# A graph layer on one core: sums stored by SyncE, a fifth of the tables resident, gathers of successive edges with narrow one-hots

## The chip, the cores and the metric

The kernel runs on one core of a Trainium2 chip. Its time is what the device takes for one execution, in microseconds (us). Eight executions of the kernel before took 15392.79 to 15410.78 us, with a median of 15401.63 us. Engines are named as in the profile: PE is TensorE (PEld its weight loads), DVE is VectorE, ACT is ScalarE, POOL is GpSimd, SP is SyncE.

## The reference, cut to what matters

```python
h = jnp.maximum(_layernorm(x, axis=-1), 0.0)           # x is [100000, 64]
local, nbr = h[dst], h[src]                            # 3.3 million edges, sorted by dst
y = concatenate([local, nbr - local]) @ W.T + b
s = segment_sum(y, dst); cnt = segment_sum(ones, dst)
out = x + where(cnt > 0, s / max(cnt, 1), 0)
```

There are 3,300,000 edges (1.6 million both ways and one loop per node), some 33 for each node. Since the layer is linear, what has to be computed per node is the sum of `h[src]` over its edges and their number. The rest is a product with the weights, node by node.

## The kernel before, in words

**First stage (L274 to L310, up to 437 us).** The layer norm is computed for 28 columns of nodes at a time. Each row of h is written as three bf16 parts and ones (194 numbers, 388 bytes) to a table in HBM, `h3` (`h` in the profile). The output's own part goes to `hb`, and zeros go to `acc`, which is to hold the sums (65 numbers a node: 64 sums and the count). `bounds` (L242) finds the smallest destination of every chunk (`base_f`, `base_b`, `base_i`, `base_r`) and flags a chunk whose destinations span 128 or more.

The edges are then summed in two ways, side by side.

**Chunks (`chunks`, L345).** A chunk is 128 x 28 successive edges of the sorted list, 28 on each partition. For each of the 28 columns POOL gathers 128 rows of `h3` by an indirect DMA (L391, `nb<-h,si`). DVE makes one-hots of the edges' destinations, 14 columns at a time and 128 wide (`one_hot`, L340, `hot<-near`), and PE multiplies them (L396, `ps<-nb,hot`), so that the 28 matmuls of a chunk sum its edges by node. DVE takes the sums to SBUF (L407, L409), and POOL adds them to `acc`: by an indirect DMA ahead of the loop (L366), by a direct one at a register's row in the loop (L371). Indices come 16 chunks at a time (`si`, `di`, L352 and L354, by SP), from which DVE makes `rel`, `near` and `to` (L356 to L361).

**Windows (`sort_lane`, `fill_lane`, `quads`).** 256 windows of 7968 edges each, of fewer than 256 nodes, are sorted by source, 128 windows at a time, one on each partition (`sort_lane`, L418: ACT copies, DVE takes minimum and maximum, L455 to L457). `fill_lane` gathers each window's pieces by source block (L636, L721) and writes the positions to HBM (`sr_d`, `dt_d`, `et_d`, `xs_d`). `quads` (L740) takes four windows at once, and 64 quads in all. A quad is 158 steps, one for each of 157 blocks of 640 nodes and one for the end. For each block:

- SP loads the table of `h3`, three blocks in one transfer of 727.5 KB (L761, `tab<-tables`, three buffers), and for each eight blocks the positions (L752 `srs`, L756 `dt`), issued eight steps ahead
- DVE makes the one-hots of two blocks at once: `gh` (L789), which picks rows out of the block, and `dh` (L340), which puts them to their nodes
- PE picks (L811, `gp<-tab,gh`, 6 matmuls a block), ACT casts the rows (L813, `gs`), PE puts them (L819, `total<-gs,dh`, 16 matmuls of 32 rows a block)

At the quad's end ACT copies the totals (L835), DVE adds the windows' own rows (L767 and L839) and reduces (L843, L845), and POOL adds four tiles of 256 nodes to `acc` (L849).

**Order.** Each engine and each queue is served in order. `chunks` is a generator: the code of the sort and of the quads takes one step of it, one gather, as often as a running account says. The account charges `GATHER` = 1250 ns for a gather and credits what the other work is taken to last: in the sort each piece's own estimate, in the four quads ahead of the loop 2 x `STEP` = 2100 ns for two steps. An addition is not issued at once but put into `later`, and issued 56 gathers after its sums are computed (`LAG`), and not sooner than `GAP` = 8 gathers after the one before it. `add_now(True)` issues all that are left.

**Loop (L909).** Four quads (`U0`) run ahead of the loop, beside `fill_lane`. The loop makes three passes of 20 quads (`SB`) and 98 chunks (`KB`). 58 chunks (`PA`) come ahead of it.

**After the loop** the flags decide on a slow path, which is not taken here (L937, L947), and the last stage reads `acc`, divides, multiplies by the weights and writes the output (L990 to L1019).

## Time and profile before, and how to read it

| | |
|---|---|
| median of 8 runs | 15401.63 us |
| profiled execution | 15381.45 us, its span 15379.7 us |
| first gather of a chunk | 437 us |
| sort, up to the first quad | 437 to 2585 us |
| four quads ahead of the loop, and the chunks left over | 2585 to 3686 us |
| the three passes of the loop start at | 3686, 7482 and 11268.5 us |
| end of the last addition in the loop | about 15050 us |
| bytes moved | 4097.9 MB, of which the tables are 3328 x 727.5 KB and 64 x 242.5 KB |

The profile shows one execution. A group is one line's instructions on one engine: their number, the time in which at least one of them ran, the mean of one, and the idle time of the engine ahead of them with what ended it. "issue" is time in which the engine waited for nothing that the profile shows. In the forty slices each digit is a share in tenths, 9 being 90% or more. The ends of matmuls are modelled, and a register load or a DMA issue does not count as busy.

### The profile page before, as it was taken

To read this page: it belongs to the slowest core of one execution; us is meant where nothing else is said; L and a number is where in the kernel's file an instruction comes from. 1 tells how busy PE (TensorE), PEld (TensorE's weight loads), DVE (VectorE), ACT (ScalarE), POOL (GpSimd) and SP (SyncE) were. 2 spreads that over 40 slices of the span, in tenths; PEclk is the share of its full clock that TensorE was granted. 3 is DMA by queue.
4 is the path that set the end of the run, shared out by engine and by line. 5 is a ranking of instruction groups with operands and counts; after the bars stand their busy time and mean duration, and the time that the engine had idled before them with its cause. 6 is when DMAs were issued, how large, how long until landed. Compare 5 with 4: busy or idle time off the path is not lost. (4 is left out here: it accounts for less than half of the span.)

```text
span 15379.7 us, 559362 instructions
## 1 busy us (share of the span) xinstructions
PE 11558.4 (75%) x238778; PEld 9478.5 (62%) x238778; DVE 11312.0 (74%) x15452; ACT 6112.6 (40%) x11710; POOL 11130.6 (72%) x11210
## 2 busy tenths in 40 slices
PE   6101001596999989998799998989979999998885
PEld 5100001475777777777677777777767777777775
DVE  6889797675777777777677777777767777777774
ACT  5335344242444444444344444444434444444441
POOL 4776766546777777777777777777777777777776
PEclk7555555798999999999899999999989999999997
DMA  7683233796999999999899999999989999999997
GB/s 295 123 104 55 48 51 76 183 311 214 319 315 308 309 304 311 309 311 305 265 310 321 314 317 304 311 307 310 308 262 310 319 313 313 313 309 308 307 306 280
DMA packets 1746424, 4097.89 MB, mean 266 GB/s; under 512 B 943899, under 2 KB 952230, under 8 KB 1738950
## 3 DMA queue, kind: packets, MB, share of 16 engines
q1 hardware_dynamic: 1182534, 3461.26, 64.7%
q0 software_dynamic: 454208, 535.92, 17.1%
q10 hardware_dynamic: 107168, 64.74, 2.4%
q8 instruction: 1877, 30.75, 0.8%
q14 instruction: 637, 5.22, 0.1%
HBM read 3880.72 MB, written 219.04 MB: 267 GB/s over the span
## 5 line engine op out<-in xcount | busy, mean ns | idle before, releaser
L391 POOL DMA_INDIRECT nb<-h,si x9856 | 9425.9, 956 | 3298.2 <-issue 2812.3
L813 ACT CAST gs<-gp 128x386 bf16<-128x386 f32 x10048 | 4837.6, 482 | 7092.0 <-PE gp L811 6867.8
L811 PE MATMUL gp<-tab,gh 128*128 128x193 bf16 x60288 | 6236.8, 251 | 989.2 <-DMA tab<-tables 614.8
L811 PEld LDWEIGHTS <-gh 128*128 128x128 bf16 x60288 | 4893.7, 99 | 2012.0 <-issue 942.4
L340 DVE TENSOR_TENSOR dh<-dt,c 128x1024 bf16<-128x1024 int16 x5056 | 3450.9, 683 | 2857.0 <-PE total L819 2726.5
L789 DVE TENSOR_TENSOR gh<-srs,c 128x1536 bf16<-128x1536 int16 x5056 | 4762.1, 942 | 19.5 <-PE gp L811 17.2
L819 PE MATMUL total<-gs,dh 32*128 32x193 bf16 x160768 | 4417.6, 247 | 36.5 <-issue 34.1
L819 PEld LDWEIGHTS <-dh 32*128 32x128 bf16 x160768 | 3196.9, 94 | 1049.3 <-issue 1029.2
L396 PE MATMUL ps<-nb,hot 128*128 128x193 bf16 x9856 | 1802.2, 263 | 2456.7 <-DVE sums L409 1876.2
L396 PEld LDWEIGHTS <-hot 128*128 128x128 bf16 x9856 | 973.7, 104 | 2433.6 <-DVE sums L409 1925.7
L455 ACT COPY tmp<-keys 128x1536 f32<-128x1536 f32 (+14 forms) x540 | 650.1, 1214 | 1239.8 <-DVE keys L457 1014.5
L456 DVE TENSOR_TENSOR keys<-tmp,keys 128x1536 f32<-128x1536 f32 (+14 forms) x540 | 756.9, 1422 | 90.6 <-ACT tmp L455 89.2
L340 DVE TENSOR_TENSOR hot<-near,c 128x1792 bf16<-128x1792 int16 x704 | 759.9, 1080 | 9.6 <-PE ps L396 9.5
L457 DVE TENSOR_TENSOR keys<-tmp,keys 128x1536 f32<-128x1536 f32 (+14 forms) x540 | 756.6, 1421 | 2.3
L849 POOL DMA_DIRECT2D acc<-wsums x256 | 348.0, 1359 | 185.1 <-DVE gh L789 62.7
L636 POOL DMA_INDIRECT kf<-ksort,at_i x322 | 310.1, 963 | 98.8 <-issue 88.9
L371 POOL DMA_DIRECT2D acc<-sums x294 | 301.8, 1027 | 15.1 <-DMA acc<-wsums 7.5
L407 DVE TENSOR_REDUCE sums<-ps 128x64 f32<-128x192 f32 x352 | 123.5, 351 | 149.1 <-PE ps L396 148.3
L839 DVE SCALAR_TENSOR_TENSOR whole<-own,whole 128x193 f32<-128x193 bf16 x512 | 191.3, 415 | 40.3 <-ACT whole L835 39.3
L303 PEld LDWEIGHTS o_ps<-w_own,hT 128*128 128x128 f32 x784 | 156.3, 254 | 79.7 <-ACT hT L298 69.8
L366 POOL DMA_INDIRECT acc<-sums,to x58 | 94.7, 1632 | 148.4 <-DVE sums L409 128.0
L721 POOL DMA_INDIRECT kx<-ksort,xat x128 | 120.8, 943 | 110.5 <-DVE xat L718 56.9
(174 smaller groups left out, 3577.7 us busy)
## 6 DMA issues: line engine op xcount, KB each, us to landing
tab<-tables SPq DMA_DIRECT2D x3328, 727.5 KB
srs<-sr_d SPq DMA_DIRECT2D x1216, 512.0 KB
nb<-h,si POOLq DMA_INDIRECT x9856
tables<-h ACTq DMA_DIRECT2D x157, 242.5 KB
h<-parts SPq DMA_DIRECT2D x28, 1358.0 KB
acc<-zeros SPq DMA_DIRECT2D x28, 910.0 KB
at<-acc SPq DMA_DIRECT2D x28, 910.0 KB
xt<-in_x SPq DMA_DIRECT2D x28, 896.0 KB
```

The lines of the kernel that those rows point to most:

```text
L340: nc.vector.tensor_tensor(out.rearrange("p k (a d) -> p k a d", d=D), numbers[:, :, None].to_broadcast(shape), upto[:shape[0], :n].rearran ...
L391: last[POOL] = nc.gpsimd.indirect_dma_start(out=nb[:, j], out_offset=None, in_=h3, in_offset=bass.IndirectOffsetOnAxis(ap=si[:, u, at:at + ...
L396: nc.tensor.matmul(ps, lhsT=before[0][:, j], rhs=before[1][:, j, :CE], start=before[2] == 0 and j == 0, stop=before[2] == parts - 1 and j ...
L455: last[ACT] = nc.scalar.copy(tmp, lo)
L456: nc.vector.tensor_tensor(lo, tmp, hi, ALU.min)
L457: last[DVE] = nc.vector.tensor_tensor(hi, tmp, hi, ALU.max)
L636: last[POOL] = nc.gpsimd.indirect_dma_start(out=kf[:, c], out_offset=None, in_=ksort, in_offset=bass.IndirectOffsetOnAxis(ap=at_i[:, c0 + ...
L789: nc.vector.tensor_tensor(gh[:, :m].rearrange("p c i b s -> p (c i) b s"), srs[u, s // SL][:, c:c + m].rearrange("p c i s -> p (c i) s")[: ...
L811: nc.tensor.matmul(gp[:, i], lhsT=ghots[t][:, i, b], rhs=row[:, b + i * (NB - NR), :CE], start=b == 0, stop=b == NR - 1)
L813: nc.scalar.copy(gs[t], gp)
L819: nc.tensor.matmul(total[:, i, to(b)], lhsT=hot[at, b * P:b * P + P], rhs=of[at], start=flags.get("start", False) and b == 0, stop=flags.g ...
L849: nc.gpsimd.dma_start(acc[ds(at, CH)].rearrange("(b p) c -> p b c", p=P), sums, accum_op=ALU.add)
```

## The change

- **Sums.** The sums of a tile of nodes are no longer added to `acc` but stored there, by SP. Two neighbouring tiles can share one node, the first of the later tile; so, ahead of the store of the next tile, SP copies that row from `acc` to a side table (`side_c`, `side_w`). After the loop the 5 tiles of side rows are added by indirect DMAs. The sums of the first three chunks (`EARLY`) stay in SBUF, and are added after the loop. `GAP` is 4.
- **Resident tables.** Every fifth table transfer (`KEEP`), 11 of 53, is made once ahead of the loop into SBUF, and the quads of the loop take these from there.
- **Gathers and one-hots.** A gather takes 128 successive edges of the sorted list (`by_gather`, on the host, which only lays out the inputs), not every 28th. Their destinations lie close together and move on by about 4 nodes a gather, so the one-hot is 32 columns wide (`BAND`), compared after the drift of 4 nodes a column is taken off, and it stands in a wider tile of zeros. PE's matmul reads 128 columns of that tile, as before. `bounds` flags a chunk whose destinations leave the band.
- **Numbers.** `KB` is 94 in place of 98, so 70 chunks come ahead of the loop in place of 58; `STEP` 1300 in place of 1050, and 350 ns more credit for each piece of the second sort (`EXTRA`); indices come 8 chunks at a time (`KG`).

The diff, cut to its core:

```diff
-KB = 98
+KB = 94
-KG = 16
+KG = 8
-STEP = 1050
-GAP = 8
+STEP = 1300
+GAP = 4
+BAND = 32
+EARLY = 3
+EXTRA = 350
+KEEP = 5
...
         def bounds(m):
             nc.vector.tensor_reduce(least[:n, m:m + 1], d[:n], axis=AX.X, op=ALU.min)
+            nc.vector.tensor_tensor(e[:n].rearrange("c (p j) -> c p j", j=J), d[:n].rearrange("c (p j) -> c p j", j=J),
+                                    drift_i[:n, None, :].to_broadcast([n, P, J]), ALU.subtract)
...
-            nc.vector.tensor_reduce(most[:n, m:m + 1], d[:n], axis=AX.X, op=ALU.max)
+            nc.vector.tensor_reduce(off[:n, 0, m:m + 1], e[:n], axis=AX.X, op=ALU.max)
...
+            nc.vector.tensor_reduce(off[:n, 1, m:m + 1], e[:n], axis=AX.X, op=ALU.min)
...
                 nc.vector.tensor_sub(rel[:, :k], di[:, :k], base_b[:, at][:, :, None].to_broadcast([P, k, J]))
+                nc.vector.tensor_sub(rel[:, :k], rel[:, :k], drift[:, None, :].to_broadcast([P, k, J]))
...
-            def addition(q, rows_to, sums):
-                if dynamic is None:
-                    nc.gpsimd.indirect_dma_start(
-                        out=acc, out_offset=bass.IndirectOffsetOnAxis(ap=rows_to, axis=0),
-                        in_=sums, in_offset=None, compute_op=ALU.add)
-                else:
-                    at = number(base_r[0:1, ds(dynamic + q, 1)], POOL, V)
-                    nc.gpsimd.dma_start(acc[ds(at, P)], sums, accum_op=ALU.add)
+            def keep(q, sums):
+                c = ds(first + q if dynamic is None else dynamic + q, 1)
+                after = ds(first + q + 1 if dynamic is None else dynamic + q + 1, 1)
+                def put():
+                    at = number(base_r[0:1, c], SP, V)
+                    last[SP] = nc.sync.dma_start(acc[ds(at, P)], sums)
+                def shared():
+                    at = number(base_r[0:1, after], SP, V)
+                    last[SP] = nc.sync.dma_start(side_c[c], acc[ds(at, 1)])
+                add_later((LAG - 1) * J, put)
+                add_later((LAG - 1) * J + GAP, shared)
+            narrow = [[few.tile([P, JH * (P + D) + JH * D], BF16, name=f"hot{part}{i}") for i in range(2)]
+                      for part in range(J // JH)]
+            for hot in narrow[0] + narrow[1]:
+                nc.vector.memset(hot, 0.0)
...
-                    hot = rows.tile([P, JH, P], BF16, name="hot", bufs=4)
+                    hot = narrow[part][q % 2]
...
-                        one_hot(hot, near[:, u, part * JH:part * JH + JH], P)
+                        one_hot(hot[:, part * JH * D:][:, :JH * (P + D)].rearrange("p (k x) -> p k x", x=P + D)[:, :, :BAND],
+                                near[:, u, part * JH:part * JH + JH], BAND)
...
-                        nc.tensor.matmul(ps, lhsT=before[0][:, j], rhs=before[1][:, j, :CE],
+                        nc.tensor.matmul(ps, lhsT=before[0][:, BAND // 2 + j * P:BAND // 2 + j * P + P], rhs=before[1][:, j, :CE],
...
-                if s < NCB and s % TG == 0:
+                if s < NCB and s % TG == 0 and kept is not None and s // TG % KEEP == 0:
+                    tabs[u, s // TG] = kept[:, s // TG // KEEP]
+                elif s < NCB and s % TG == 0:
...
-                    def addition(w=(base + u) * W + i, sums=sums):
-                        at = number(wb_r[0:1, ds(w, 1)], POOL, V - CH)
-                        nc.gpsimd.dma_start(acc[ds(at, CH)].rearrange("(b p) c -> p b c", p=P), sums, accum_op=ALU.add)
-                    add_later((LAG - 1) * J, addition)
+                    keep(u, i, sums)
+            def keep(u, i, sums):
...
+                def put():
+                    at = number(wb_r[0:1, w], SP, V)
+                    last[SP] = nc.sync.dma_start(acc[ds(at, CH)].rearrange("(b p) c -> p b c", p=P), sums)
+                def shared():
+                    at = number(wb_r[0:1, after], SP, V + P)
+                    last[SP] = nc.sync.dma_start(side_w[w], acc[ds(at, 1)])
+                add_later((LAG - 1) * J, put)
+                add_later((LAG - 1) * J + GAP, shared)
...
-                        gathers(ns)
+                        gathers(ns + (EXTRA if l else 0))
...
+                kept = stay.tile([P, -(-NTB // KEEP), TG, NB, CT], BF16, name="kept")
+                for k in range(0, NTB, KEEP):
+                    m = min(TG, NCB - k * TG)
+                    nc.sync.dma_start(kept[:, k // KEEP, :m].rearrange("p c b f -> p (c b f)"),
+                                      tables[k][:, :m].rearrange("p c x -> p (c x)"))
...
-                    for _ in quads(U0 + g * SB, SB):
+                    for _ in quads(U0 + g * SB, SB, kept):
...
+                for q, sums in enumerate(early):
+                    at = number(base_r[0:1, q:q + 1], POOL, V)
+                    nc.gpsimd.dma_start(acc[ds(at, P)], sums, accum_op=ALU.add)
...
+        for k in range(SETS * W // P):
+            add_side(k, side_w, wb_d, 0, P)
+        for k in range(NMT):
+            add_side(k, side_c, base_i.rearrange("m p -> (m p)")[:, None], 0 if k else EARLY, min(P, NCH - 1 - k * P))
```

`add_side` loads 128 side rows and their nodes, and adds them to `acc` by one indirect DMA of POOL. Small checks of the tiles' order go into the flags (a handful of DVE instructions on one partition).

## The prediction

> **What bounds the kernel now.** I read the page first, then one pass of the loop by groups and by waits, then a few microseconds of it in order of time.
>
> The page: the share of each engine, then forty slices of the span.
>
> ```profile
> span 15379.7 us, 559362 instructions
> PE 11558.4 (75%) x238778; PEld 9478.5 (62%) x238778; DVE 11312.0 (74%) x15452; ACT 6112.6 (40%) x11710; POOL 11130.6 (72%) x11210
> ...
> DMA  7683233796999999999899999999989999999997
> ```
>
> No engine is above 75%, and yet the DMA row stands at 9 from the eleventh slice on: that is the loop (L909), three passes over 20 quads each, from 3686 us to about 15050 us, 11364 us of 15380. A pass is bounded by what never stops in it, so I took the middle one, from its first gather at 7482 us to the first gather of the next at 11268.5 us, and its groups on POOL (count, then busy us, mean ns, then idle us ahead of them):
>
> ```profile
> L391 POOL DMA_INDIRECT nb<-h,si x2744 | 2617.4, 954 | 847.6 <-issue 780.7 <-DMA nb<-h,si 21.3 <-PE gp L811 18.3
> L849 POOL DMA_DIRECT2D acc<-wsums x80 | 108.6, 1357 | 56.7 <-DMA acc<-wsums 20.2 <-DVE dh L340 17.7 <-DVE gh L789 16.2
> L371 POOL DMA_DIRECT2D acc<-sums x98 | 100.7, 1028 | 4.9 <-DMA acc<-wsums 2.4 <-DVE sums L409 2.3
> L778 POOL DMA_INDIRECT rows_x<-h,xs x40 | 38.6, 965 | 12.2 <-issue 11.9 <-DMA nb<-h,si 0.3
> ```
>
> Busy and idle of these four groups add to 3786.7 us, the whole pass: POOL never waits for anybody (the idle before a gather is 0.3 us of its own issue), so 72% busy is POOL at its limit. One gather costs (2617.4 + 847.6 - 12.0 for the one wait on its indices) / 2744 = 1.258 us.
>
> PE is the neighbour. The waits of the same pass (us in total, times, longest):
>
> ```profile
> PE gp L811 <- DMA tab<-tables: 175.2, 198, 3.6
> PE ps L396 <- DMA nb<-h,si: 113.1, 68, 40.7
> ...
> DVE rel L356 <- DMA di<-in_dst_p: 42.4, 7, 8.2
> ...
> PE ps L396 <- DVE sums L409: 34.7, 43, 3.0
> ...
> PE gp L811 <- DVE gh L789: 27.0, 12, 6.1
> ```
>
> PE is busy 3388.9 of the 3786.5 us. It waits for POOL's gathers only 113 us, 41 of them once, at the top of the pass. So if POOL were free, PE would gain some 72 us inside the pass and no more: the two are nearly tied, and what the change gives PE counts as much as what it takes from POOL. PE's rows in order of time (start, length):
>
> ```profile
> 6009.81 1.15 PE L811 MATMUL gp<-tab,gh 128*128 128x193 bf16 x6 [3.06 <-DMA tab<-tables]
> ...
> 6012.47 2.12 PE L811 MATMUL gp<-tab,gh 128*128 128x193 bf16 x12
> ...
> 6015.89 1.19 PE L811 MATMUL gp<-tab,gh 128*128 128x193 bf16 x12
> ...
> 6017.96 1.19 PE L811 MATMUL gp<-tab,gh 128*128 128x193 bf16 x12
> ...
> 6020.03 1.19 PE L811 MATMUL gp<-tab,gh 128*128 128x193 bf16 x12
> ...
> 6022.02 1.19 PE L811 MATMUL gp<-tab,gh 128*128 128x193 bf16 x12
> ```
>
> Undisturbed, two steps take 2.07 us (1.99 with one chunk matmul among them instead of two): 1580 pairs at about 2.05 are 3239 us, PE's floor in a pass. The row at 6012.47 is stretched from 1.19 to 2.12 us because DVE put a chunk's one-hot between the two it makes for PE; DVE's own row, with its 1.08 us:
>
> ```profile
> 6013.19 1.08 DVE L340 TENSOR_TENSOR hot<-near,c 128x1792 bf16<-128x1792 int16 x1
> ```
>
> **The change, part by part, for one pass.**
>
> Sums. The 80 + 98 additions leave POOL: 108.6 + 56.7 + 100.7 + 4.9 = 271 us. Four chunks fewer are 112 gathers, 141 us. POOL is left with 2632 x 1.258 = 3311, rows_x 51, the 12 us on the indices, together 3374 us, and what follows the last gather. There the seven last additions now run one after the other, each waiting for the one before, from 11234.3 to 11256.4 us: 22 us, 3.2 each. In their place stand two transfers for each sum, a store and a copy of the next tile's first row out of the same tensor, on SP, each behind the other: 14 x 3.2 = 44 us. POOL's sum is 3418 us.
>
> On SP a sum costs two register loads and two issues. The own-row loads (L767) have the same form and follow each other every 1.28 us, so 348 items are 445 us of SP, which is busy with its instructions about a quarter of the loop and otherwise waits for PE to free a table buffer. Queued behind a waiting store or copy are the table, srs, dt and index loads, and PE waits for the tables. A copy must wait until its store has landed, the next store until the copy has. Bounds: nothing, if each wait falls into SP's idle time (items are at least 4 gathers, 5.0 us, apart, and an addition lands in about 3.2 us); 3.2 + 1.28 us for every item, 1559 us, if none does. I take 25 us, because the spacing is longer than the landing.
>
> The Trainium skill, "DMA: Bandwidth & Descriptors", section Queues, rings and completion order, says that a queue's descriptors are taken in ring order on each engine. It speaks against this part: POOL's additions had a queue of their own, and the stores line up behind the tables. A table of 727.5 KB at the 307 GB/s of this pass takes 2.4 us, so by that rule an item lands after some 5.6 us, not 3.2, and the 5.0 us of spacing leaves 0.6 us x 348 = 209 us of SP waiting in a pass. The trace of before has no such store, so it cannot decide.
>
> Tables. 33 of 157 blocks stay (11 of 53 loads of a quad): 20 x 33 x 242.5 KB = 164 MB of the pass's 1161, 14%. Three buffers of three steps each mean that a load may take two tables' time, 6 steps or 6.2 us; a resident table among them makes it 9.3 us, and that holds for three loads of four. Of the 42 loads left in a quad about 10.5 keep the short cover, against 53 now: 175.2 x 10.5 / 53 = 35 us. Bounds 0 and 175; I take 45.
>
> The Trainium skill, "TensorE: Matmul & The Clock Gate", section Part 1: The HAM clock gate, has an idle array run at half rate until about 3.4 us of work have passed. The row at 6009.81 fits: after 3.06 us of idle six matmuls take 1.15 us, which take 0.68 elsewhere. By that rule each long table wait that goes would give back up to 1.7 us more; I add nothing for it.
>
> One-hots. The rows of the same helper are 683 ns for 1024 columns, 1080 for 1792 and 1480 for 2560, so about 0.52 ns a column and 150 ns fixed; 14 x 32 = 448 columns are 0.38 us. DVE then makes dh, gh and hot in 0.68 + 0.94 + 0.38 = 2.0 us, inside PE's 2.05. The stretch of 2.12 - 1.19 = 0.93 us goes, 196 times: at most 182 us, at least nothing, since DVE catches up in the next pair; half, 91. The sums that stand behind a hot come sooner: of 34.7 us 20 go, of the 27 on gh 17.
>
> Chunks. 112 matmuls fewer at 0.08 us are 9. Index loads double in number, 7 to 12, at 6 us of wait each (42.4 / 7), half the bytes: +25 us. The order of edges inside a gather changes neither its count nor its bytes.
>
> PE's sum: busy 3388.9 - 9 - 91 = 3289. Idle is 398 now; tables -130, gathers -72, sums -20, gh -17, index +25 leave 184. With 22 us more at the pass's end: 3495. POOL has 3418, so **PE is late next**. I add the 25 us for SP: **3520 us a pass**, against 3788 on the mean now: 3 x 268 = -804 us.
>
> Before the loop. 336 gathers more, 423 us of POOL. The 58 indirect additions go (95 us busy, 148 idle ahead of them on the page): -243. In the first four quads POOL waits 224 us for PE's buffers, and the larger STEP puts gathers there. That leaves -44. DVE, which is 89% busy in the sort, saves 85 x 0.70 us less 13 new at 0.38, 54 us, and spends some 25 us more on the bounds at the start. I take -30; from -110 to +120, if the gathers left over at the end of the quads (195 us by their number, 156) don't overlap.
>
> After the loop: three additions kept back and five indirect ones for the first rows, each behind the other at 3.2 us, with their loads: 8 x 3.2, and some 20 us for loads and small DVE work: +45 us. The resident tables are loaded in the first quads, 8 MB, where DMA has room: 0.
>
> Sum: 15381.45 us of the profiled execution (its span 15379.7) - 30 - 804 + 45 = 14592. The median of the eight runs is 20 above that execution: **14610 us**.
>
> **The rivals.**
>
> POOL stays the bound (chance 0.17). For it: its row has no idle at all, and PE's waits may shrink more than I take. Then a pass is 3418 us, 102 less than mine: 14300 us.
>
> The cover doesn't pay (0.15). SP's new work in front of the tables eats the longer cover, and the one-hots' stretch was caught up anyway. PE keeps 175 us on tables and the 91: 3520 + 130 + 91 = 3741 less what POOL's tie no longer adds, about 3700: 15150 us. Against it: the DMA row loses 14% of its bytes.
>
> SP becomes the chain (0.15), the way to a slower kernel. Store and copy alternate on one in-order queue with the tables behind them. If an item delays a table by more than 268 / 348 = 0.77 us on the mean, and PE feels it, the gain of a pass is gone. At 1.5 us it is 522 a pass instead of 25: 3520 + 497 = 4017, 16100 us. Against it: SP idles three quarters of the loop.
>
> No difference (0.03): the gains and SP's delay cancel. That the change isn't in force is excluded: the program of the changed kernel has no addition of POOL in the loop and 14 x 32 columns in its one-hots.
>
> **The numbers.** My forecast has 0.50, by itself 14400 to 14900. A difference of 0.2% (31 us) is about what a measurement of this kernel can tell. Faster: 0.50 + 0.17 + 0.15 = 0.82; same 0.03; slower 0.15. The range takes in the first three: 14250 to 15300.
>
> **What would show it.** Right: no POOL addition in the loop, POOL with waits on PE's buffers (nb <- PE ps) of some 100 us a pass, hot at 0.38 us, table waits under 60 us a pass, pairs still at 2.07 us. Wrong: SP rows that wait long on acc; table waits as before or larger; POOL still without idle; or a gather that no longer costs 1.258 us, from which half of my sum hangs.

## The result, and the profile after

The changed kernel takes 15436.49 us (median of 12 runs, 15392.53 to 15489.95), the kernel before 15399.64 us (33 runs beside them, 15388.63 to 15410.92): a ratio of **1.0024, 95% interval 1.0017 to 1.0031**. I had said 14610. Where the 0.24% comes from, stage by stage, from the two spans:

| stage | before, us | after, us | difference | forecast |
|---|---|---|---|---|
| up to the first pass of the loop | 3686.5 | 3974.9 | +288 | -30 |
| three passes | 11364 | 11082 (3684.5, 3696.8, 3700) | -282 | -804 |
| after the loop | 330 | 355 | +25 | +45 |
| span | 15379.7 | 15411.7 | +32 | -789 |

So the change does bring something in each pass, 94 us and not 268, and loses all of it ahead of the loop. The page of the changed kernel, engines and slices:

```profile
span 15411.7 us, 562939 instructions
PE 11531.1 (75%) x238778; PEld 9533.2 (62%) x238778; DVE 10917.2 (71%) x15549; ACT 6106.8 (40%) x11710; POOL 10315.1 (67%) x10611
...
DMA  7494223686688888888788888888878888888887
```

POOL went from 72% to 67%, and the DMA row in the loop from 9 to 8: both reliefs came. The middle pass (7659.4 to 11356.2 us), POOL's gathers of the chunks (count, then busy us, mean ns, then idle us ahead of them and what ended it):

```profile
L424 POOL DMA_INDIRECT nb<-h,si x2632 | 2484.5, 944 | 1139.4 <-issue 760.2 <-DMA si<-in_src_p 145.3 <-PE gp L849 134.7
```

Beside these POOL has only the 40 rows_x. The additions are gone, and POOL, which waited for nobody before, now waits for its indices and for PE. It is not the bound any more: its last gather of the pass ends at 11259.0 us, 66 us ahead of PE's last quad (11325.5). Before, it ended 12 us behind it (11234.3 and 11222.0). PE's waits in the same pass (us in total, times, longest):

```profile
PE gp L849 <- DMA tab<-tables: 185.9, 122, 6.5
PE gp L849 <- DVE gh L827: 46.2, 24, 5.7
```

The first line matters most. A fifth of the tables is never loaded, and still PE waits for tables 186 us, against 175. It waits less often (122 times, not 198) and longer at a time (6.5 us, not 3.6). For the gathers it waits 45 us (113 before), for the sums 20 (35). Who holds the loads up stands in the waits of SP's own queue in that pass:

```profile
SPq L799 <- PE gp L849: 859.9, 478, 6.4
SPq L788 <- DVE gh L827: 581.6, 263, 10.3
...
SPq L396 <- DMA acc<-sums: 105.4, 43, 5.4
SPq L893 <- DMA side_w<-acc: 101.6, 35, 5.0
SPq L897 <- DMA acc<-wsums: 48.6, 31, 4.2
```

The first line before:

```profile
SPq L761 <- PE gp L811: 1686.6, 828, 12.6
```

This wait is harmless: a table load (L799) that waits for PE to free the buffer is a load that is early. Spread over 840 loads in place of 1061, SP's lead fell from 1.6 to 1.0 us a load. The second is a load of `srs` that waits for its buffer, 447 us before; rival R-b below is about it. The last three are new: a copy that waits for its store to land, and a store for its copy, 109 waits and 256 us a pass. One of the longest table waits, SP's queue in order of time:

```profile
9031.59 0.92 SPq L897 DMA_DIRECT2D side_w<-acc  x1
9037.82 0.42 SPq L893 DMA_DIRECT2D acc<-wsums  x1
9038.29 1.92 SPq L799 DMA_DIRECT2D tab<-tables  x2
```

and PE beside it:

```profile
9037.58 0.68 PE L849 MATMUL gp<-tab,gh 128*128 128x193 bf16 x6
9044.75 1.15 PE L849 MATMUL gp<-tab,gh 128*128 128x193 bf16 x6 [6.50 <-DMA tab<-tables]
```

A copy is issued until 9032.5 us. The store behind it waits until 9037.8 us for the copy's 260 bytes to land, 5.3 us, one of the longest such waits. Two table loads stand behind that store and go out at 9038.3 us and after, and PE, which reached the table at 9038.3, gets it at 9044.75.

### The profile page after: what moved, and what is told of

Same layout as the page of the kernel before. It is cut to its first block, busy times and chain, and to the rows that moved or that the text cites. A ratio compares the mean times of both kernels' runs of the same rounds, so it can differ in the third digit from the quotient of the medians.

```text
span 15411.7 us, 562939 instructions
## 1 busy us (share of the span) xinstructions
PE 11531.1 (75%) x238778; PEld 9533.2 (62%) x238778; DVE 10917.2 (71%) x15549; ACT 6106.8 (40%) x11710; POOL 10315.1 (67%) x10611
## 5 line engine op out<-in xcount | busy, mean ns | idle before, releaser
L849 PE MATMUL gp<-tab,gh 128*128 128x193 bf16 x48408 | 5055.5, 252 | 1112.5 <-DMA tab<-tables 690.6
L849 PE MATMUL gp<-kept,gh 128*128 128x193 bf16 x11880 | 1241.2, 249 | 6.9 <-DVE gh L827 3.6
L363 DVE TENSOR_TENSOR hot<-near,c 128x448 bf16<-128x448 int16 x704 | 267.7, 381 | 76.5 <-PE ps L429 76.4
L321 PE MATMUL o_ps<-w_own,hT 128*128 128x128 f32 x784 | 196.7, 388 | 16.2 <-ACT hT L316 15.5
L305 POOL TENSOR_TENSOR sq<-xt,parts 128x1792 f32<-128x1792 f32 x28 | 98.6, 3525 | 162.7 <-ACT parts L304 162.7
L1106 DVE TENSOR_TENSOR yt<-y_ps,ht 128x512 f32<-128x512 f32 x112 | 65.5, 620 | 176.5 <-POOL ht L1093 122.7
```

Source lines behind the costliest of these rows:

```text
L321: nc.tensor.matmul(o2[:, i], lhsT=hT[:, i], rhs=w_own.rearrange("p a c -> p (a c)"), start=False, stop=True)
L363: nc.vector.tensor_tensor(out.rearrange("p k (a d) -> p k a d", d=D), numbers[:, :, None].to_broadcast(shape), upto[:shape[0], :n].rearran ...
L849: nc.tensor.matmul(gp[:, i], lhsT=ghots[t][:, i, b], rhs=row[:, b + i * (NB - NR), :CE], start=b == 0, stop=b == NR - 1)
```

## The experiments

Theory T1: in the loop, the stores and copies stand in SP's program ahead of the table loads and delay them, which takes away what the resident tables give. (Comparing in the traces, load by load, when PE's last matmul freed the buffer with when SP issued: in the loop of the kernel before 9% of the loads came more than 0.2 us late, by 0.25 us on the mean over all; in the changed one 40%, and 1.2 us.) The rivals: R-a, the short cover of a load next to a resident table makes the waits; R-b, a load of `srs` or `dt` that waits for its buffer does; R-c, the waits are only where PE shows slack that POOL sets. For the loss ahead of the loop: the order in which gathers are issued, or their number, or the one-hots and checks.

Of 18 runs 13 fell on chips where the kernel before took 24511 to 24857 us in place of 15375 to 15384, and there PE waited on its own issue; the last section tells of them. Their times do not bear on the theories. The readings that follow are from the other five. The rows are from the middle pass of each.

**1. The sums back on POOL, all else as changed.**

```diff
-                    at = number(wb_r[0:1, w], SP, V)
-                    last[SP] = nc.sync.dma_start(acc[ds(at, CH)]..., sums)
+                    at = number(wb_r[0:1, w], POOL, V)
+                    nc.gpsimd.dma_start(acc[ds(at, CH)]..., sums, accum_op=ALU.add)
...
-                add_later((LAG - 1) * J + GAP, shared)
```

(the same for the chunks; `GAP` is 8 again, and no side rows are added after the loop)

> The changed kernel, but the sums are added by GpSimd as before: no stores and no copies on SyncE in the loop, no side rows after it, GAP 8. Resident tables, narrow one-hots and the numbers stay. Theory T1 (the store and copy items stand in SyncE's queue ahead of the table loads, so that 41% of the loads are issued late and the waits on tables stay at 186 us a pass): the waits gp<-tab fall to 60 us a pass or less, and GpSimd, which gets 271 us back, becomes the bound at 3374 + 271 = about 3650 us a pass, 50 less than the 3700 of the changed kernel; total 15436 - 150 - 20 (nothing after the loop) + some 20 for the 70 indirect additions ahead of the loop that GpSimd cannot hide = about 15300. Rival R-a (the waits belong to the shorter cover of the load that stands last before a resident table, and to the landing time itself): the waits stay at 150 to 190 us, as in both kernels. Rival R-b (a load of srs or dt that waits for its buffer at the head of the queue holds the tables): the waits stay at 150 or more.

There it took 24702.85 us, 0.9933 of the kernel before, and nothing follows. Run again:

> The same kernel as in e4_pool_sums (the changed kernel with the sums added by GpSimd as before), because the chip of that run took 24857 us for the kernel before, with TensorE waiting on its own issue, and so could not tell the theories apart. The expectation is unchanged: T1 has the waits gp<-tab at 60 us a pass or less and GpSimd as the bound at about 3650 us a pass, total about 15300; R-a and R-b have the waits on tables at 150 to 190 us. If TensorE waits on its issue again, nothing follows.

15202.27 us, ratio 0.9885 (0.9868 to 0.9901); passes 3622 and 3626 us. PE's wait on tables in the second:

```profile
PE gp L844 <- DMA tab<-tables: 13.9, 21, 2.4
```

and POOL's groups in the same pass:

```profile
L419 POOL DMA_INDIRECT nb<-h,si x2633 | 2511.8, 954 | 818.9 <-issue 748.1 <-DMA nb<-h,si 21.6 <-DMA si<-in_src_p 17.8
L888 POOL DMA_DIRECT2D acc<-wsums x80 | 109.0, 1363 | 43.0 <-DVE gh L822 16.9 <-DMA acc<-wsums 10.6 <-DVE hot L363 4.6
L392 POOL DMA_DIRECT2D acc<-sums x94 | 96.5, 1026 | 4.9 <-DMA acc<-wsums 2.5 <-DVE sums L438 2.2
```

Table waits fall from 186 to 14 us, and 7% of the loop's loads are issued more than 0.2 us late, not 40%: resident tables do pay when no item stands ahead of the loads. R-a and R-b would have kept the waits; both are out as the main cause (the loads of `srs` even wait longer for their buffer, 677 us in the pass). With rows_x (51 us) POOL's rows add up to the pass again, to within 9 us, and its last gather ends 12 us behind PE's last quad: POOL is the bound, as forecast (3650), and PE waits 159 us for gathers. A gather costs (2511.8 + 818.9 - 17.8) / 2633 = 1.258 us, as before. Note what this pass says of the tables: of the 160 us it is shorter than before, 141 are the 112 gathers that were moved out of it. Where POOL is the bound, 160 us less waiting for tables buys next to nothing.

**2. A fourth table buffer, and STEP 1800.** Two edits in one kernel. STEP acts ahead of the loop alone; the fourth buffer serves the loop and the four quads ahead of it.

```diff
-                    tabs[u, s // TG] = tab = load.tile([P, TG, NB, CT], BF16, name="tab")
+                    tabs[u, s // TG] = tab = load.tile([P, TG, NB, CT], BF16, name="tab", bufs=4)
-STEP = 1300
+STEP = 1800
```

> The changed kernel with two edits that act in different stages: four table buffers in place of three (the loop), and STEP 1800 in place of 1300 (the four quads ahead of it). Loop: T1 has a table loaded 3.1 us sooner, so that a delay of 1.0 us on the mean in SyncE's queue no longer reaches TensorE: waits gp<-tab under 60 us a pass in place of 186, pass 3540 to 3600 in place of 3700. If the waits stay above 120, the delays are far longer than their mean or the table stands behind a waiting srs or dt; if the waits go and the pass falls by less than 40 us, something else bounds it, GpSimd's waits for index loads (145 us) before all. Ahead of the loop: a credit of 3600 ns for two steps puts 158 more gathers, 2 to 3 a pair instead of 1.4, beside the quads, and the 264 us after the quads fall to under 100, while the quads grow by less than 100 us: the loop starts at 3840 to 3930 in place of 3975. If the quads grow by as much as the rest shrinks, GpSimd and not the order of issue is what the part costs. Total 15436 - 375 - 90 = about 14970.

**14811.98 us, ratio 0.9628 (0.9612 to 0.9644)**: the fastest kernel of this study, faster than both. The loop starts at 3774.8 us, sooner than expected (3840 to 3930), and the passes are 3552 and 3558.5 us. PE's wait on tables in the second:

```profile
PE gp L849 <- DMA tab<-tables: 48.6, 39, 3.2
```

SP still stores and copies, and 51% of the loop's loads are issued late; they are only free to go out 3 us sooner, and the table waits fall to 49. R-c is out, since the pass does follow: 138 us for 137, though not one for one, as PE's other idle time grows by 32 us and its busy time falls by 33. PE is the bound here: 3320.6 busy of 3558.5, and its last quad ends 50 us behind POOL's last gather.

Ahead of the loop the account shows in POOL's gathers between the first quad and the loop, first in the changed kernel, then in this one:

```profile
L424 POOL DMA_INDIRECT nb<-h,si x612 | 578.8, 946 | 414.5 <-PE ps L429 216.3 <-issue 175.3 <-DMA nb<-h,si 11.1
```

```profile
L424 POOL DMA_INDIRECT nb<-h,si x611 | 579.8, 949 | 223.1 <-issue 173.1 <-PE ps L429 30.5 <-DMA nb<-h,si 14.9
```

The same gathers, but POOL's waiting for PE to free gather buffers went from 216 to 31 us. In the changed kernel POOL waited beside the quads, and 196 gathers were left to make by itself after PE's last `gp` matmul of the four quads at 3718.6 us, up to 3964.5. With STEP 1800 they are 4. The quads themselves, from their first to their last `gp` matmul, take 1089 us in place of 1067. The account was charged for the 225 gathers of `fill_lane` too, so that 316 pairs of 2600 ns gave only 316 x 2600 / 1250 - 225 = 432 gathers of chunks; at 3600 ns they are 685, more than there are.

**3. No resident tables, all else as changed.**

```diff
-                    for _ in quads(U0 + g * SB, SB, kept):
+                    for _ in quads(U0 + g * SB, SB):
```

(the eleven loads ahead of the loop go too)

> The changed kernel without resident tables: all 53 loads of a quad are made again, through three buffers; everything else as changed. T1 (items in SyncE's queue hold up the loads, and the longer cover of three loads of four takes part of that): every load now has the cover of 6.2 us only, and 53 are issued behind the same 348 items in place of 42, so the waits gp<-tab rise from 186 to 300 to 450 us a pass and the pass from 3700 to 3810 to 3950, above the 3788 of the kernel before; total 15436 + 3 x 180 = about 15980. If the resident tables were the cause themselves (the load next to one has the short cover), the waits fall under 150 and the pass under 3700. If the loads held for nothing, as the kernel before has 175 with 53 loads and no items, the waits stay at 175 to 200 and the pass at 3700.

> The changed kernel without resident tables, again, since its first run fell on a chip where TensorE waited on its issue (24819 us for the kernel before). Unchanged: T1 expects the waits gp<-tab at 300 to 450 us a pass in place of 186 and a pass of 3810 to 3950 in place of 3700, total about 15980; waits under 150 and a pass under 3700 would say that the resident tables make the waits; waits of 175 to 200 and a pass of 3700 that they did nothing.

Both on those chips: 25781.35 and 25544.56 us, ratios 1.0386 and 1.0425. The third time:

> The changed kernel without resident tables, a third time; the first two fell on chips on which TensorE waited on its issue, where table waits do not show. Unchanged: T1 expects the waits gp<-tab at 300 to 450 us a pass in place of 186 and a pass of 3810 to 3950 in place of 3700, total about 15980; waits under 150 and a pass under 3700 would say that the resident tables make the waits; waits of 175 to 200 and a pass of 3700 that they did nothing.

16173.75 us, ratio 1.052 (1.0503 to 1.0538); passes 3941 and 3961 us. PE's wait on tables in the second:

```profile
PE gp L849 <- DMA tab<-tables: 379.6, 270, 5.3
```

As T1 had it (300 to 450 us), though the second pass came out 11 us above its range and the whole run 194 us above the 15980. So the two parts of the change stand against each other: with the items on SP, and all tables loaded, the table waits are double those of the kernel before (175 to 380); the resident tables halve them again (to 186). R-a has the wrong sign.

**4. The items on ScalarE's queue, three table buffers, STEP 1800.** Is it the items' transfers that hold the tables up, or their place in SP's program?

```diff
-                    at = number(wb_r[0:1, w], SP, V)
-                    last[SP] = nc.sync.dma_start(acc[ds(at, CH)]..., sums)
+                    at = number(wb_r[0:1, w], ACT, V)
+                    last[ACT] = nc.scalar.dma_start(acc[ds(at, CH)]..., sums)
```

(and so the other three)

> The changed kernel with the stores and copies issued by ScalarE on its own queue (three table buffers, as changed) and STEP 1800. If the items hold the tables up because they stand in SyncE's program (T1), the waits gp<-tab fall from 186 to under 60 us a pass; if it is the transfers themselves (their bytes and the landing they wait for, whoever issues them), the waits stay at 150 or more. ScalarE then issues 348 items a pass, of 0.4 to 0.9 us and a register load each, among its casts gs, and waits for landings there: on the slow chip TensorE waited 216 us a pass for gs with this edit. So TensorE is expected to wait 100 to 250 us a pass for gs in place of tables: pass 3560 + 100 to 200 = 3640 to 3760, total 15000 to 15350. The loop starts at about 3775 as with STEP 1800 elsewhere.

26225.33 us there, ratio 1.0563. Again:

> The changed kernel with the stores and copies issued by ScalarE on its own queue (three table buffers) and STEP 1800, again, since its first run fell on a chip where TensorE waited on its issue. Unchanged: waits gp<-tab under 60 us a pass if the items hold the tables up by standing in SyncE's program, 150 or more if their transfers do it, whoever issues them; 100 to 250 us a pass of waits for the casts gs; pass 3640 to 3760, total 15000 to 15350.

17042.26 us, ratio 1.109 (1.1072 to 1.1109); passes 4283 and 4252.5 us. PE's waits, then ScalarE's:

```profile
PE gp L849 <- ACT gs L851: 612.8, 177, 9.0
...
PE gp L849 <- DMA tab<-tables: 15.2, 21, 2.6
```

```profile
ACT gs L851 <- DMA side_c<-acc: 554.3, 80, 10.8
ACT gs L851 <- DMA side_w<-acc: 273.7, 60, 7.5
```

It fits the place. The same stores and copies move, and the table waits are 15 us, with 5% of the loads late. Alone this run would not settle it, since PE is so much slower here that the tables have more time; experiment 1, with a shorter pass, is the firmer ground. By their size the transfers count for little: 80 stores of 65 KB and 94 of 32.5 KB are under 1% of a pass's 991 MB. But the casts now stand behind the items, 828 us of idle ahead of them in a pass (some 340 of these are the items' own instructions), and PE waits 613 us for them. I had expected 100 to 250, from the 216 us of the run told of next, and missed by far; the loop, too, starts at 3864 us, not 3775. The same edit with STEP 1300 fell on one of the chips told of below:

> The changed kernel, but the stores and the copies of the shared rows are issued by ScalarE on its own queue; SyncE keeps only loads. T1: the waits gp<-tab fall from 186 to 60 us a pass or less, as without the items. What ScalarE does with them is not in any trace: if an item's issue and its wait for the one before delay the casts gs, TensorE waits for gs instead (total<-gs). 348 items of 0.9 to 1.3 us lie within ScalarE's idle 60%; a wait on the landing of the one before (up to 3 us) would hold a cast beyond its pair. Pass between 3560 (nothing felt) and 3560 + 348 x 1.0 = 3900; value taken 3620, total 15200. R-a and R-b: the waits on tables stay at 150 to 190.

It gave 26293.39 us, ratio 1.0573 there, with 10 us of table waits and some 216 us of waits for casts a pass; no verdict.

**5. Four table buffers, STEP 1800 and KB 96.**

```diff
-KB = 94
+KB = 96
```

(against the kernel of experiment 2)

> The changed kernel with four table buffers, STEP 1800, and KB 96 in place of 94 (64 chunks ahead of the loop, not 70: 168 gathers fewer there, 56 more in each pass). With KB 94 the loop started at 3775 us and a pass was 3552 us. If the number of gathers is what is left of the loss ahead of the loop (3775 against 3686 in the kernel before), 168 x 1.25 us = up to 210 us can go, and the loop starts at 3600 to 3680; if the wider checks at the start and the narrow one-hots make it, it stays above 3740. In the loop GpSimd has 3311 + 70 + 67 for rows_x and the end = 3448 us of its own and waits 140 to 170 us for its index loads in SyncE's queue: if these waits overlap with its slack, a pass grows by 5 to 30 us; if not, it is bound by GpSimd at about 3620. Total between 14812 - 130 + 40 = 14720 and 14812 - 100 + 200 = 14910; value taken 14760.

15027.34 us, ratio 0.977 (0.9754 to 0.9787); the loop starts at 3754.1 us, passes 3646 and 3638. A miss in both stages. With 168 gathers fewer the loop starts only 21 us sooner, so the number of gathers is not what is left of the loss there: POOL's last one ends at 3526.7 us, and POOL then waits 227 us for the loop's first indices, while PE's four quads go on to 3729.5. They take 1083 us, against 965 in the kernel before; why is not shown. And in the loop the pass grew by 79 to 94 us, not 5 to 30. PE's wait on tables in the second pass:

```profile
PE gp L849 <- DMA tab<-tables: 113.7, 49, 6.3
```

That is 65 us more than in experiment 2, and PE is 36 us longer busy. POOL now waits 217 us a pass for its index loads, which stand in SP's queue behind the items as well, but 91 of these are the end of the pass: its last gather ends at 10946.8 us, 61 us ahead of PE's last quad (11008.3). So POOL is not the bound, though the pass comes near the 3620 that I had for that case. Why 56 gathers more bring the table waits back is not shown.

**6. Not settled.** Three kernels gave results only on the other chips: four table buffers alone, the old numbers (KB 98, STEP 1050, EXTRA 0), and the changed kernel without the copies of the shared rows and their additions (its sums are incomplete where two tiles share a node).

> The changed kernel with four table buffers in place of three. T1: a table may be loaded 9.3 us ahead, 12.4 beside a resident one, so a delay of 1.0 us on the mean in SyncE's queue no longer reaches TensorE; the waits gp<-tab fall from 186 to under 30 us a pass, and a pass from 3700 to about 3540 to 3580 (the waits on ps and gh, 45 each, stay); total 15436 - 3 x 140 = about 15020. Rival R-a expects the same of the waits (cover is longer either way), so this run does not tell T1 from R-a; it tells what the waits are worth. Rival R-c (the table waits are only where TensorE shows its slack; the pass is set by GpSimd and the pairs): the waits move to ps<-nb or gh and the pass falls by less than 40 us. Rival R-b: the queue is stopped by srs and dt, so the waits stay above 100 us.

> The changed kernel with four table buffers in place of three, again, since its first run fell on the chip where TensorE waited on its issue. With the sums back on GpSimd the waits gp<-tab fell to 14 to 26 us a pass, so R-a and R-b are out as the main cause, and T1 stands. T1 here: a fourth buffer lets a table be loaded 3.1 us sooner, so that a delay of 1.0 us on the mean in SyncE's queue no longer reaches TensorE: waits gp<-tab under 60 us a pass in place of 186, pass 3540 to 3600, total 15436 - 3 x 125 = about 15060. If the waits stay above 120, the delays in the queue are far longer than their mean, or the table in turn stands behind a waiting srs or dt. If the waits go and the pass falls by less than 40 us, GpSimd's waits for its index loads (145 us a pass, also behind the items on SyncE) have become the bound.

25514.94 and 25500.09 us, ratios 1.0264 and 1.0267, with the waits on issue of the others on those chips.

> The changed kernel with the numbers of the kernel before: KB 98 (58 chunks ahead of the loop, not 70), STEP 1050, EXTRA 0. Theory for the loss ahead of the loop (the 336 gathers more do not fit beside the sort and the quads: four quads +98 us, the gathers left at their end +127, the sort +38): the loop begins at about 3700 us or earlier in place of 3975, since GpSimd has also lost its 58 indirect additions there. In the loop 112 gathers more make 141 us of GpSimd's time; T1 has GpSimd waiting 280 us a pass there, so a pass grows by 10 to 50 us only: 15436 - 275 + 3 x 30 = about 15250. Rival (gathers still pace the loop): a pass grows by 141, total 15436 - 275 + 423 = about 15585. Rival for the part ahead of the loop (the narrow one-hots or the new bounds make it long, not the number of gathers): the loop begins at 3900 or later.

> The changed kernel with KB 98, STEP 1050 and EXTRA 0 as before, again, since its first run fell on the chip where TensorE waited on its issue. Unchanged: the loop begins at about 3700 us or earlier in place of 3975 if it is the number of gathers that makes the part ahead of the loop long, at 3900 or later if it is the narrow one-hots or the bounds. A pass grows by 10 to 50 us if SyncE's delays set it, total about 15250; by 141 if the gathers set it, total about 15585.

25654.52 and 25638.37 us, ratios 1.0316 and 1.0321. On those chips the loop starts at 4263 to 4270 us with the old numbers, and at 4614 to 4673 in the kernels with KB 94 and STEP 1300.

> The changed kernel without the copies of the shared rows and without the side tables' additions after the loop (so the sums of nodes that two tiles share are incomplete); the stores stay. SyncE has 174 items a pass in place of 348, and a store waits for no copy and no copy for it. Of the lateness of the table loads in the changed kernel's trace, the copies' own issue makes 180 us a pass (0.92 each), the waits of copies on stores some 95, half of the 156 for registers; the stores' side has 93 of waiting for copies, 75 of issue and the other half of the registers. T1: the waits gp<-tab fall from 186 to 50 to 110 us a pass, the pass from 3700 to about 3620; after the loop some 16 us less; total 15436 - 3 x 80 - 16 = about 15180. If it is the stores alone (their bytes, 130 KB each for a window, in front of the tables), the waits stay above 150; if it is the copies alone, they fall under 40, as without any item.

> The changed kernel without the copies of the shared rows and without the side tables' additions after the loop (the sums of nodes that two tiles share are incomplete), again, since its first run fell on a chip where TensorE waited on its issue. Unchanged: T1 expects the waits gp<-tab at 50 to 110 us a pass in place of 186, a pass at about 3620 in place of 3700, total about 15180; over 150 if the stores alone hold the tables, under 40 if the copies alone do.

> The changed kernel without the copies of the shared rows and without the side tables' additions after the loop (the sums of nodes that two tiles share are incomplete), a third time; the first two fell on chips on which TensorE waited on its issue. T1 expects the waits gp<-tab at 50 to 110 us a pass in place of 186, a pass at about 3620 in place of 3700, total about 15180; over 150 if the stores alone hold the tables, under 40 if the copies alone do.

> The changed kernel without the copies of the shared rows and without the side tables' additions after the loop (the sums of nodes that two tiles share are incomplete), once more; the earlier runs fell on chips on which TensorE waited on its issue. T1 expects the waits gp<-tab at 50 to 110 us a pass in place of 186, a pass at about 3620 in place of 3700, total about 15180; over 150 if the stores alone hold the tables, under 40 if the copies alone do.

25202.88, 25328.59, 25368.53 and 25375.09 us, ratios 1.0269, 1.0217, 1.0219 and 1.0219.

Experiment 2 answers the first in place of it. The second would have shown the part ahead of the loop with fewer gathers; experiment 5 answers that in part. The third would have told how the table waits divide between stores and copies. That stays open. (Its expectation has 130 KB for a window's store; the traces have 65 KB.)

## Why the prediction was wrong, point by point

The forecast of the span was 14591 us, the span 15411.7: 821 us too little. Ahead of the loop 318, in the loop 3 x 174 = 522, after it -20.

- **The failed step in the loop** is the one on SP: "I take 25 us, because the spacing is longer than the landing." The landing of 3.2 us was read from POOL's additions, which had POOL's queue to themselves (those start 3.2 to 3.8 us after one another, 3.5 on the mean, so it was also read a little low). On SP 109 of the 348 items wait for the landing of the one before, by 2.3 us on the mean and up to 5.4: 256 us a pass. And the items' own instructions, which I had laid into SP's idle time, make SP's instructions 1398 us a pass in place of 966. The price is not paid where I put it, in a term of its own, but in the table waits: 186 in place of 45, 141 us. How these divide between landings and instructions is not shown.
- The Trainium skill, "DMA: Bandwidth & Descriptors", section Queues, rings and completion order, was quoted against this part. Worked out from its ring order, the estimate was that an item lands after 5.6 us and SP waits 209 us a pass. The direction was right, and the 256 us are near; but they come from a third of the items at 2.3 us, not from all at 0.6. In the DMA records of the changed kernel's middle pass a copy's last packet has moved 2.4 us after its issue, in the median (0.8 to 7.1, the end of the pass left out). On ScalarE's queue, with no tables in it, it is 0.7 (0.4 to 4.4). A window's stores show the same (3.5 and 1.7), a chunk's do not (3.3 and 3.9).
- **The table term** is not contradicted: with no item on SP (14 us, but POOL is the bound there) and with a fourth buffer (49 us) the waits lie on both sides of the 45 that I took. No run has three buffers, no items and PE as the bound.
- PE's busy time: 3289 expected, 3354 found, 65 more. DVE's `hot` costs 381 ns as worked out (0.38 us), but of the half of the stretch, 91 us, only 26 came off: PE's busy time fell by 35 us, of which 9 are matmuls. In experiment 2 it fell by 68. The granted clock has a part in that, for which the prediction added nothing: after the wait of 6.50 us above it is 0.50 from 9044.75 to 9047.57 us, and the six matmuls take 1.15 us, not 0.68. PE was busy at a clock of 0.5 for 163 us of the pass (157 before) and for 102 in experiment 2; half of the difference is 30 of the 33 us between these two. Why the stretch gave less than half was not tried.
- `gh`: 46 us of waits, where I had 27 - 17 = 10. Lateness from the tables is not the reason: in experiment 2, with a quarter of the table waits, they are 65. What makes them is not shown.
- 25 us for the index loads and 22 for the pass's end did not show in PE's waits. 141 + 65 + 36, less these and the 25 for SP, are 170 of the 174.
- **The failed step ahead of the loop:** "the larger STEP puts gathers there. That leaves -44." It put too few there, because the gathers of `fill_lane` are charged to the same account. From the first quad to the loop took 224 us more than before; the kernel with STEP 1800 and four table buffers gave 202 of them back. That STEP moves the gathers shows with three buffers too: in experiment 4 none is left after the quads, though these take 1217 us with the items on ScalarE. I had read the constant and not the sum it feeds. My bound of +120 had the gathers left over in it, 156 of them; there were 196 after the quads, and PE had ended.
- Up to the first quad it took 64 us more: 26 in the first stage (I had 25), and 38 in the sort, where I had -54. DVE's busy time did fall by 52 us in the sort, but it waited 132 us for the gathers `kf` on POOL, where it had waited 7, and 52 for `xs`, where it had 36; one wait of 96 us for POOL's `lo` went. POOL made 94 gathers of chunks more in that stretch. What DVE saved was not on the path; that the gathers took it is argued, not shown.
- After the loop +25 against +45: the eight additions run one after the other from 15056.7 to 15080.9 us, 24 us to the start of the last, about as taken (8 x 3.2); the 20 us for loads and small work did not show.
- **POOL:** 271 us of additions and 112 gathers left it, as said, and it stopped being the bound. That was right, and with PE late next as well. That the passes of experiment 2, 3552 and 3558.5 us, are close to the forecast 3520 is in part luck: its fourth buffer was not in the forecast.
- **The rivals.** "The cover doesn't pay" had SP's new work in front of the tables eating the longer cover, and about 3700 us a pass: the mechanism and the number (3694 on the mean), though its second half, a stretch that was caught up anyway, came true only in part. It missed the 318 us ahead of the loop. "SP becomes the chain" needed more than 0.77 us of delay felt by PE for each item; measured, 186 - 49 = 137 us for 348 items are 0.4. On ScalarE, 613 / 348 = 1.8 us, it did decide.

## What to carry to other kernels

A transfer that waits for another to land is priced with the landing time on the queue that it will stand in, and with everything that stands behind it in that engine's program; "the engine is idle three quarters of the time" does not price it, since the lead of the loads behind it is only a few us. Where such items must stay ahead of prefetches, one more buffer for the prefetch can buy the delay back (here 137 us a pass, of which 65 were gone again with 56 gathers more in the pass). And a pacing constant is read together with everything that is charged to its account, before it is taken to hide work.

## What the runs showed of the hardware that I had not expected

- A 260-byte copy from HBM to HBM holds SP for 0.92 us, and ScalarE in experiment 4 for 1.3; a store of a window's sums holds either for 0.4.
- On ScalarE the waits put down to the same landings are longest at 10.8 us and 828 us a pass, the items' own instructions included; on SP 5.4 and 256. ScalarE's order leaves less time between two items: half of them start within 4.7 us of the one before (7.1 on SP), and 146 of 337 have no cast between them. In the longest a copy is next in line behind its store and goes out 8.4 us after it.
- Thirteen runs fell on chips on which the kernel before takes 24511 to 24857 us. There PE waits on "issue", that is for nothing that the profile shows; PE's costliest group in one pass of the kernel without copies on such a chip:

```profile
L856 PE MATMUL total<-gs,dh 32*128 32x193 bf16 x50240 | 1912.6, 262 | 1250.0 <-issue 1246.0 <-ACT whole L872 1.2
```

With the 785 us ahead of the `gp` matmuls it is over 2000 us of "issue" a pass, against 34 in the changed kernel's pass above, and 11 us of waits on tables. The granted clock is 0.75 in that pass (0.97 in the changed kernel's above), and whether that is the cause or comes of the idle time is not shown. The chip's number in the record does not tell: under number 7 the kernel before took 24511, 15376 and 24833 us. The order of the kernels is another one there: sums on POOL 0.993, without copies 1.022 to 1.027, four buffers 1.026 and 1.027, the old numbers 1.032, no resident tables 1.039 and 1.043, items on ScalarE 1.056 and 1.057. Where PE's own instructions come late, there are hardly any table waits left to save. Why they come late is not shown by any run here.
